# The last two token tiles of a time-mix and GELU-FFN kernel by column halves, and the first block's output projection behind its FFN

## The chip, the cores and the metric

The kernel runs on one core of a Trainium2 chip. The metric is the device time of one execution in microseconds (us). Before the change the median of 3 runs is 937.84 us (937.31 to 937.91).

## What is computed

The input x is 4 sequences of 1024 tokens with 512 channels. It is layer-normalised, and two branches work on the normalised tokens. Their results are added to x.

```python
xn = _layernorm(x, axis=-1)
# branch 1: time mix, with a running state per hidden unit (704 of them)
xx = concatenate([xn[:, 1:2, :], xn[:, :-1, :]], axis=1) - xn
k = einsum('btc,hc->bth', xn + xx * time_mix_k, Wk)
r = einsum('btc,hc->bth', xn + xx * time_mix_r, Wr)
w = exp(-exp(time_decay))
state_t = state_(t-1) * w + relu(k_t);   out_t = state_t * r_t
out = einsum('bth,ch->btc', out, Wv)
attn = (out - mean) * rsqrt(var + 1e-5) * ln_gamma + ln_beta
# branch 2: FFN, hidden size 2048, inner values rounded to float16
D = gelu(xn.astype(float16) @ W0.T + bias0).astype(float16)
E = (D @ W1.T + bias1).astype(float16)
x + attn + E
```

## The kernel before

**Tiling.** The 4096 tokens are cut into 8 blocks of 512 (`TB`), two per sequence. A block has NS = 4 token tiles of 128. The 704 hidden units of the time mix are five full chunks of 128 and one half chunk of 64. The FFN's 2048 hidden units are NN = 16 chunks of 128. The weights W0 and W1 are each held as a sum of two reduced-precision parts (w0h and w0l, and the two halves of a w1 tile), so each product with them is two matmuls.

**The stages of a block.** `full_chunks` (L398) makes, for each full chunk, the products pk and pr (L222), the state by a scan on DVE (L386) after a Relu on ACT (L384), and the gated value g (L412). `half_chunk` (L418) makes both products of the half chunk in 64x64 quarters of the array (L430, the sum called pkr), brings them to SBUF on DVE as kr (L438, L439), then Relu, scan and gh (L442). `attention_out` (L451) is the output projection: per token tile five matmuls with g (L459) and the half matmuls with gh (L470, also 64x64), all into the sums po. Its `residual` then takes statistics, normalises, and adds the residual xres, giving z (L478 to L490). It has a hook `amid`, called between the half matmuls and the second part of the full ones. `ffn` (L519) makes for each chunk n the up product pd (`up`, 8 matmuls, L529), the GELU on ACT (L537), a cast on DVE to d (L539), and the down product into the four sums pe (`down`, 8 matmuls, L545). Up products run AHEAD = 2 chunks in front of the down products. `rounded` (L508) adds bias1 to pe and rounds to float16; `finish` (L514) adds that to z and stores it.

**Order across blocks.** TensorE's order is the program's. The main loop (L603 to L646) runs the FFN of block i. The dictionary `between` names what is inserted in front of a chunk: the projection of the same block in front of chunk 0 where `within` holds (L626: the first block and the last), the layernorm of block i+1 in front of chunk 4, its transposes and mixing in front of chunk 7 or 9. Because the two up products of `waiting` come first (L570), an inserted projection stands between the up products of chunks 1 and 2. For the blocks that are not `within`, the projection stands behind the FFN, and the half chunk of the next block is made in its `amid` hook (L642). For block 1 the half chunk is made after its full chunks (L646), since the projection of block 0 is already done. The half chunk of block 0 is made ahead of the loop (L602).

**Weights and queues.** In front of the first FFN the 16 pieces of W0 are loaded through three buffers tagged "raw" and split: ACT copies the high part (L134), DVE subtracts for the low part (L135). During the first FFN the chunks of W1 take the same way through the same three buffers and are also kept in DRAM (L164); later blocks load them from there (L168). All large loads and stores are issued on SP in the order of its queue. Instructions on ACT, DVE, POOL and SP are placed by a scheduler that follows the program's priorities; a few stages fix their own order by hand (`manual_schedule`), among them the start (L294) and the end (L581).

**The end.** In the last block the last four chunks' down products are held back (`last = 4`). Token tiles 0 to 2 are then finished one after the other. The last tile's sum over the first twelve chunks is put to SBUF with the bias (`base`, L583), and the rest of its sum is made by two halves of 256 columns, each with its own PSUM sum, rounding, addition and store (`end_by_columns`, L553).

Of the kernel before, what the change touches and what calls it, by code (L numbers as in the profile page):

```python
# [8 lines left out]
F16 = mybir.dt.float16  # L9
F32 = mybir.dt.float32  # L10
# [4 lines left out]
P = 128  # L15
# [4 lines left out]
def time_mix_and_gelu_ffn(  # L20
# [26 lines left out]
    nc = tc.nc  # L47
    B, T, C = x.shape
    HID = wkT.shape[1]
    N = w0T.shape[1]  # L50
    TB = 512
    NS = TB // P
    NC = C // P
    NN = N // P
# [9 lines left out]
    def pool(name, bufs, **kw):  # L64
        return ctx.enter_context(tc.tile_pool(name=name, bufs=bufs, **kw))
# [6 lines left out]
    two = pool("two", 2)  # L72
    three = pool("three", 3)
    four = pool("four", 4)
    ps_mm = pool("ps_mm", 4, space=bass.MemoryType.PSUM)
# [55 lines left out]
    b1_sb = const.tile([P, C], F32, name="b1_sb")  # L131
# [11 lines left out]
    def load_w0(g):  # L143
        for c in range(NC):
            raw = three.tile([P, W0G], F32, tag="raw", name=f"w0raw_{g}_{c}")
            cols = slice(g * W0G, (g + 1) * W0G)
            nc.sync.dma_start(raw, w0T[c * P : (c + 1) * P, cols])
            split(w0h[c][:, cols], w0l[c][:, cols], raw)

    def load_w1(i, n):  # L150
        if i == len(blocks) - 1 and n == NN - 1:

            parts = [
                three.tile([P, C], F32R, tag="raw", name=f"w1_{i}_{n}_{p}") for p in range(2)
            ]
            for p in range(2):
                nc.sync.dma_start(parts[p].bitcast(F32), w1_dram[n][:, p, :].bitcast(F32))
            return parts
        w1 = wide.tile([P, 2, C], F32R, tag="w1", name=f"w1_{i}_{n}", bufs=3)
        if i == 0:  # L160
            raw = three.tile([P, C], F32, tag="raw", name=f"w1raw_{n}")
            nc.sync.dma_start(raw, w1T[n * P : (n + 1) * P, :])
            split(w1[:, 0, :], w1[:, 1, :], raw)
            kept = nc.sync.dma_start(w1_dram[n].bitcast(F32), w1.bitcast(F32))  # L164
            if n == NN - 1:
                state["kept"] = kept
        else:
            nc.sync.dma_start(w1.bitcast(F32), w1_dram[n].bitcast(F32))  # L168
        return [w1[:, p, :] for p in range(2)]
# [12 lines left out]
    last = const.tile([P, NC, 1], F32, name="last")  # L182
# [187 lines left out]
    def ffn_input(i, x16s):  # L370
        xf = wide.tile([P, NC, TB], F32R, tag="xf", name=f"xf_{i}")
        for c in range(NC):
            nc.vector.tensor_copy(xf[:, c, :], x16s[c])
        return xf
# [133 lines left out]
    def rounded(i, s, pe):  # L508

        e16 = four.tile([P, C], F16, tag="e16", name=f"e16_{i}_{s}")  # L510
        nc.vector.tensor_add(e16, pe, b1_sb)  # L511
        return e16

    def finish(i, s, z, e16, cols=slice(0, C)):  # L514
        b, t0 = blocks[i]
        state["added"] = nc.vector.tensor_add(z[:, cols], z[:, cols], e16)  # L516
        nc.sync.dma_start(out[b, t0 + s * P : t0 + (s + 1) * P, cols], z[:, cols])

    def ffn(i, xf, between, state):  # L519


        pe = [ps_e.tile([P, C], F32, tag="pe", name=f"pe_{i}_{s}") for s in range(NS)]

        def up(n):
            pd = ps_mm.tile([P, TB], F32, tag="mm", name=f"pd_{i}_{n}")
            cols = slice(n * P, (n + 1) * P)
            for c in range(NC):
                for w in (w0h, w0l):
                    nc.tensor.matmul(  # L529
                        pd,  # L530
                        w[c][:, cols],
                        xf[:, c, :],
                        start=(c == 0 and w is w0h),
                        stop=(c == NC - 1 and w is w0l),
                    )
            d16 = two.tile([P, TB], F16, tag="d16", name=f"d16_{i}_{n}")
            state["gelu"] = nc.scalar.activation(d16, pd, AF.Gelu, bias=b0_sb[:, n : n + 1])  # L537
            d = wide.tile([P, TB], F32R, tag="d", name=f"d_{i}_{n}", bufs=4)
            nc.vector.tensor_copy(d, d16)  # L539
            return d  # L540

        def down(n, s, d, w1, first=0, end=NN, sum_=None, cols=slice(0, C)):

            for part in range(2):
                nc.tensor.matmul(  # L545
                    pe[s] if sum_ is None else sum_,
                    d[:, s * P : (s + 1) * P],
                    w1[part][:, cols],
                    start=(n == first and part == 0),
                    stop=(n == end - 1 and part == 1),  # L550
                )

        def end_by_columns(s, chunks, z):  # L553


            first = NN - len(chunks)
            for half in range(2):
                cols = slice(half * C // 2, (half + 1) * C // 2)
                sum_ = ps_mm.tile([P, TB], F32, tag="mm", name=f"end_{half}")[:, : C // 2]
                for n, operands in chunks:  # L560
                    down(n, s, *operands, first=first, sum_=sum_, cols=cols)
                e16 = four.tile([P, C], F16, tag="e16", name=f"e16_end_{half}")[:, : C // 2]
                nc.vector.tensor_add(e16, sum_, state["base"][:, cols])  # L563
                finish(len(blocks) - 1, s, z, e16, cols)

        last = 4 if i == len(blocks) - 1 else 0
        AHEAD = 2
        waiting = [(up(n), load_w1(i, n)) for n in range(AHEAD)]  # L570
        for n in range(NN):
            if n in between:
                between[n]()
            if n + AHEAD < NN:
                waiting.append((up(n + AHEAD), load_w1(i, n + AHEAD)))
            if n < NN - last:
                operands = waiting.pop(0)
                for s in range(NS):
                    down(n, s, *operands, end=NN - last if s == NS - 1 else NN)
        if last:  # L580
            with tc.manual_schedule(engines={nc.tensor.engine, nc.vector.engine}):  # L581
                chunks = list(zip(range(NN - last, NN), waiting))
                state["base"] = two.tile([P, C], F32, tag="xx", name="base")  # L583
                nc.vector.tensor_add(state["base"], pe[NS - 1], b1_sb)
                for s in range(NS - 1):
                    for n, operands in chunks:
                        down(n, s, *operands)
                    finish(i, s, state["zs"][s], rounded(i, s, pe[s]))
                end_by_columns(NS - 1, chunks, state["zs"][NS - 1])
        return pe  # L590

    state = {}
    behind = ExitStack()
    first_x16s, xk, pks = first_inputs(x_now, behind)

    full_chunks, half_chunk = attention(0, xk, pks)
# [4 lines left out]
    for i in range(len(blocks)):  # L603
        more = i + 1 < len(blocks)
        if i == 0:
            for grp in range(N // W0G):
                load_w0(grp)
            behind.close()
            load_late_constants()
        if more:  # L610

            with tc.issue_after(state["kept"].ins) if i == 1 else nullcontext():
                x_now = load_x(i + 1)

        def out_stage():
            state["zs"] = attention_out(i, g, gh)

        def next_norm():
            with tc.issue_after(added.ins) if added else nullcontext():
                layernorm(i + 1, x_now)  # L620

        def next_inputs():
            transposed(x_now)
            state["mixed"] = mixed_inputs(i + 1, state["gelu"])

        within = i == 0 or not more  # L626
        added = state.get("added")
        between = {0: out_stage} if within else {}
        if more:
            between[4] = next_norm  # L630
            between[9 if i == 0 else 7] = next_inputs
        pe = ffn(i, xf, between, state)
        if more:
            x16s, xk = state["mixed"]
            e16s = [rounded(i, s, pe[s]) for s in range(NS)]
            xf = ffn_input(i + 1, x16s)
            full_chunks, half_chunk = attention(i + 1, xk)
            next_gh = []
            if within:
                zs = state["zs"]  # L640
            else:
                zs = attention_out(i, g, gh, lambda: next_gh.append(half_chunk()))  # L642
            for s in range(NS):
                finish(i, s, zs[s], e16s[s])
            g = full_chunks()
            gh = next_gh[0] if next_gh else half_chunk()  # L646
# [43 lines left out]
```

## The time and the profile before

| | us |
|---|---|
| median of 3 runs | 937.84 |
| profiled execution, whole | 937.6 |
| its span, first to last instruction | 935.5 |
| TensorE busy (matmul) | 930.3 |
| DVE busy | 500.7 |
| ACT busy | 164.4 |
| POOL busy | 55.6 |

The profiled execution has 9338 instructions, and the granted clock of TensorE reads 1.000. The views used are these. The first part of the page gives busy time, share of the span and number of instructions of each engine. The chain of waits in order of time follows the work that ended last back from the end; each line has a start, a length, the engine and the line of the program. The timeline of one engine shows start, length, engine, line, operation, output and inputs, how many instructions were merged, and in brackets the idle time ahead of it and what ended it. A line of the waits names who waited for whom, and then the total in us, the number of times and the longest. The table of windows gives busy time by stretches of the span.

The matmuls of the stages cost, in the chain: pd 24.9% of the span, pe 24.7%, po 14.8% (L459) and 1.6% (L470), pk 14.8%, pr 14.7%, pkr 3.0%.

### The profile page before, as it was taken

The numbers are of one execution on the slowest core, as the hardware profiler recorded it, in microseconds if no ns is written. First come the engines' busy times: TensorE is split into PE (matmuls) and PEld (weight loads), VectorE is DVE, ScalarE is ACT, GpSimd is POOL, SyncE is SP. The second block draws the span as 40 slices with busy tenths as digits, with TensorE's granted clock in tenths as the row PEclk, the third lists the DMA queues.
The fourth block names the chain that finished last, engine by engine and source line by source line (L and its number), as shares of the span: only waits on it lengthen the run. The fifth ranks groups of instructions, "written<-read, shape, count | busy, mean of one in ns | idle before, by whom it ended". The sixth has DMA issues, their size and how long they took to land.

```text
span 935.5 us, 9338 instructions
## 1 busy us (share of the span) xinstructions
PE 930.3 (99%) x3513; PEld 593.2 (63%) x3513; DVE 500.7 (54%) x875; ACT 164.4 (18%) x273; POOL 55.6 (6%) x130
## 2 busy tenths in 40 slices
PE   9999999999999999999999999999999999999998
PEld 8448854885448854588545884458844688445686
DVE  6678772833846338463484535755257552552513
ACT  5423410220002200112001220112100121001021
POOL 1010000000100001000010000100001000000100
PEclk9999999999999999999999999999999999999999
DMA  9654660443204432054320543105431044310243
GB/s 299 208 169 158 225 224 1 139 155 113 90 0 158 144 105 90 0 171 145 100 80 0 180 143 118 55 1 192 146 113 46 15 143 146 102 45 1 67 157 114
DMA packets 40296, 106.53 MB, mean 114 GB/s; under 512 B 4511, under 2 KB 5820, under 8 KB 40252
## 3 DMA queue, kind: packets, MB, share of 16 engines
q1 hardware_dynamic: 40192, 105.92, 34.1%
q8 instruction: 28, 0.46, 0.2%
q14 instruction: 16, 0.13, 0.0%
q10 hardware_dynamic: 60, 0.02, 0.0%
HBM read 89.14 MB, written 16.78 MB: 113 GB/s over the span
## 4 chain that ended last, share of the span: by engine, by line
PE 99%; DVE 0%; POOL 0%; issue 0%; POOLq 0%
PE pd L529 25%; PE pe L545 25%; PE po L459 15%; PE pk L222 15%; PE pr L222 15%; PE pkr L430 3%; PE po L470 2%; PE idle L243 1%; PE pt L261 0%; DVE z L516 0%; DVE e L511 0%; DVE e_end L563 0%; POOL ident masks.py:199 0%; PE small L300 0%; POOL ident masks.py:197 0%
## 5 line engine op out<-in xcount | busy, mean ns | idle before, releaser
L545 PE MATMUL pe<-w,d 128*128 128x512 f32 x1016 | 248.6, 389 | 0.0
L545 PEld LDWEIGHTS pe<-w,d 128*128 128x128 f32 x1016 | 190.6, 188 | 40.1 <-issue 0.4
L529 PE MATMUL pd<-xf,w0h 128*128 128x512 f32 x512 | 202.8, 396 | 0.0
L529 PE MATMUL pd<-xf,w0l 128*128 128x512 f32 x512 | 199.3, 389 | 0.0
L539 DVE CAST d<-d 128x512 fp32r<-128x512 f16 x128 | 54.2, 424 | 185.7 <-ACT d L537 184.3
L537 ACT ACTIVATE d<-pd,small_sb 128x512 f16<-128x512 f32 x128 | 87.8, 687 | 345.4 <-PE pd L529 345.4
L222 PE MATMUL pk<-xk,wk 128*128 128x512 f32 (+1 forms) x392 | 144.8, 515 | 0.0
L222 PE MATMUL pr<-xnT,wr 128*128 128x512 f32 x320 | 143.7, 592 | 0.0
L459 PE MATMUL po<-wv_sb,g 128*128 128x512 f32 x320 | 140.8, 595 | 0.0
L222 PEld LDWEIGHTS pk<-xk,wk 128*128 128x128 f32 x392 | 67.5, 190 | 70.6 <-issue 70.4
L529 PEld LDWEIGHTS pd<-xf,w0h 128*128 128x128 f32 x512 | 96.1, 188 | 23.3 <-issue 2.7
L529 PEld LDWEIGHTS pd<-xf,w0l 128*128 128x128 f32 x512 | 96.1, 188 | 21.7 <-issue 1.9
L222 PEld LDWEIGHTS pr<-xnT,wr 128*128 128x128 f32 x320 | 60.5, 189 | 76.4 <-issue 76.2
L459 PEld LDWEIGHTS po<-wv_sb,g 128*128 128x128 f32 x320 | 60.1, 190 | 76.0 <-issue 75.4
L216 DVE STREAM_TRANSPOSE xnT<-x 32x512 f32<-32x512 f32 x112 | 78.7, 702 | 2.0
L384 ACT ACTIVATE rk<-pk 128x512 f32<-128x512 f32 x40 | 23.9, 597 | 229.9 <-PE pk L222 229.4
L195 DVE BATCH_NORM_STATS2 sty<-po 128x6 f32<-128x512 f32 x32 | 22.0, 689 | 61.6 <-PE po L470 60.0
L386 DVE TENSOR_TENSOR_SCAN st<-small_sb,carry,rk 128x512 f32<-128x512 f32 (+1 forms) x24 | 30.7, 1280 | 41.9 <-ACT rk L384 41.9
L412 DVE TENSOR_TENSOR g<-st,pr 128x512 f32<-128x512 f32 x40 | 27.4, 684 | 35.3 <-PE pr L222 34.7
L386 DVE TENSOR_TENSOR_SCAN st<-small_sb,rk 128x512 f32<-128x512 f32 (+1 forms) x24 | 29.2, 1218 | 29.1 <-ACT rk L384 29.1
L189 POOL TENSOR_SCALAR ry<-mvy 128x1 f32<-128x1 f32 x32 | 11.5, 358 | 432.4 <-DVE mvy L196 432.4
L384 ACT ACTIVATE rk<-kr 64x512 f32<-64x512 f32 x8 | 5.0, 630 | 146.4 <-DVE kr L439 146.4
(70 smaller groups left out, 489.9 us busy)
## 6 DMA issues: line engine op xcount, KB each, us to landing
w<-w1d SPq DMA_DIRECT2D x111, 512.0 KB, 3.3
x<-in_L_attn_x SPq DMA_DIRECT2D x32, 256.0 KB, 3.4
xres<-in_L_attn_x SPq DMA_DIRECT2D x32, 256.0 KB, 2.7
w1d<-w SPq DMA_DIRECT2D x16, 512.0 KB, 2.9
out<-z SPq DMA_DIRECT2D x31, 256.0 KB, 2.5
w0raw<-in_L_ffn_W SPq DMA_DIRECT2D x16, 256.0 KB, 3.7
w1raw<-in_L_ffn_W SPq DMA_DIRECT2D x16, 256.0 KB, 3.4
wr<-in_L_attn_Wr SPq DMA_DIRECT2D x4, 352.0 KB, 5.3
```

What stands on the lines that cost most here:

```text
L195: nc.vector.bn_stats(st6, src)
L216: nc.vector.transpose(dst[i * Q : (i + 1) * Q, :, :, j, :], src[j * Q : (j + 1) * Q, :, :, i, :],)
L222: return nc.tensor.matmul(dst, w[c][:, cols], src, start=(c == 0), stop=(c == NC - 1))
L384: nc.scalar.activation(rk[:hw], pk, AF.Relu)
L386: nc.vector.tensor_tensor_scan(st[:hw], w_sb[:hw, h : h + 1].to_broadcast([hw, TB]), rk[:hw], 0.0 if t0 == 0 else carry[:hw, h : h + 1], A ...
L412: nc.vector.tensor_mul(g[:, h, :], st, pr)
L430: nc.tensor.matmul(out_, w[c][rows, H0:], src, start=(c == 0), stop=(c == NC - 1),)
L459: nc.tensor.matmul(pos[s], g[:, h, s * P : (s + 1) * P], wv_sb[:, h, :], start=(first and h == 0), stop=(not first and h == NF - 1),)
L529: nc.tensor.matmul(pd, w[c][:, cols], xf[:, c, :], start=(c == 0 and w is w0h), stop=(c == NC - 1 and w is w0l),)
L537: state["gelu"] = nc.scalar.activation(d16, pd, AF.Gelu, bias=b0_sb[:, n : n + 1])
L539: nc.vector.tensor_copy(d, d16)
L545: nc.tensor.matmul(pe[s] if sum_ is None else sum_, d[:, s * P : (s + 1) * P], w1[part][:, cols], start=(n == first and part == 0), stop=( ...
```

## The change

There are three edits. `within` becomes `not more`, so the projection of block 0 is no longer inserted into its FFN; it follows it, as for blocks 1 to 6, with the half chunk of block 1 in its `amid` hook. In the last block, tiles 2 and 3, and no longer tile 3 alone, get a base in SBUF and are finished by column halves. And `finish` can store its columns in several parts; tiles 0 and 1 of the last block are stored in two.

```diff
-    def finish(i, s, z, e16, cols=slice(0, C)):
+    def finish(i, s, z, e16, cols=slice(0, C), stores=1):
         b, t0 = blocks[i]
         state["added"] = nc.vector.tensor_add(z[:, cols], z[:, cols], e16)
-        nc.sync.dma_start(out[b, t0 + s * P : t0 + (s + 1) * P, cols], z[:, cols])
+        width = (cols.stop - cols.start) // stores
+        for c0 in range(cols.start, cols.stop, width):
+            part = slice(c0, c0 + width)
+            nc.sync.dma_start(out[b, t0 + s * P : t0 + (s + 1) * P, part], z[:, part])
...
-        def end_by_columns(s, chunks, z):
+        def end_by_columns(s, chunks, base, z):
...
-                nc.vector.tensor_add(e16, sum_, state["base"][:, cols])
+                nc.vector.tensor_add(e16, sum_, base[:, cols])
...
+        by_columns = range(NS // 2, NS) if last else ()
...
-                    down(n, s, *operands, end=NN - last if s == NS - 1 else NN)
+                    down(n, s, *operands, end=NN - last if s in by_columns else NN)
         if last:
             with tc.manual_schedule(engines={nc.tensor.engine, nc.vector.engine}):
                 chunks = list(zip(range(NN - last, NN), waiting))
-                state["base"] = two.tile([P, C], F32, tag="xx", name="base")
-                nc.vector.tensor_add(state["base"], pe[NS - 1], b1_sb)
-                for s in range(NS - 1):
-                    for n, operands in chunks:
-                        down(n, s, *operands)
-                    finish(i, s, state["zs"][s], rounded(i, s, pe[s]))
-                end_by_columns(NS - 1, chunks, state["zs"][NS - 1])
+                bases = {}
+                for s in by_columns:
+                    bases[s] = two.tile([P, C], F32, tag="xx", name=f"base_{s}")
+                    nc.vector.tensor_add(bases[s], pe[s], b1_sb)
+                for s in range(NS):
+                    z = state["zs"][s]
+                    if s in by_columns:
+                        end_by_columns(s, chunks, bases[s], z)
+                    else:
+                        for n, operands in chunks:
+                            down(n, s, *operands)
+                        finish(i, s, z, rounded(i, s, pe[s]), stores=2)
...
-        within = i == 0 or not more
+        within = not more
```

The scheduler reorders other engines in consequence. On DVE the layernorm of block 1 moves to between the splits of W0, and the 16 transposes of block 1's input begin between the two instructions that make kr of block 0; the projection's DVE work of block 0 moves behind the FFN. On ACT the order at the start of the first FFN stays: the splits of W0, three of W1, the Relu of the half chunk, the load of the table, the GELUs. On TensorE three up products of block 0 now stand ahead of the first down product. On SP the loads of xres for tiles 2 and 3 of block 0 move behind the FFN.

More of the change, by code (lines that the diff above doesn't have):

```diff
@@ L558, in end_by_columns @@
                 cols = slice(half * C // 2, (half + 1) * C // 2)
-                sum_ = ps_mm.tile([P, TB], F32, tag="mm", name=f"end_{half}")[:, : C // 2]
+                sum_ = ps_mm.tile([P, TB], F32, tag="mm", name=f"end_{s}_{half}")[:, : C // 2]
                 for n, operands in chunks:
                     down(n, s, *operands, first=first, sum_=sum_, cols=cols)
-                e16 = four.tile([P, C], F16, tag="e16", name=f"e16_end_{half}")[:, : C // 2]
-                nc.vector.tensor_add(e16, sum_, state["base"][:, cols])
+                e16 = four.tile([P, C], F16, tag="e16", name=f"e16_{s}_{half}")[:, : C // 2]
+                nc.vector.tensor_add(e16, sum_, base[:, cols])
                 finish(len(blocks) - 1, s, z, e16, cols)
         last = 4 if i == len(blocks) - 1 else 0
+        by_columns = range(NS // 2, NS) if last else ()
         AHEAD = 2
```

## The prediction

> **What bounds the kernel now.** I read the page's first part, then the chain of waits in order of time, then the table of windows by block, then the timelines of ACT and DVE around the first FFN, then SP's waits. The engine shares:
>
> ```profile
> PE 930.3 (99%) x3513; PEld 593.2 (63%) x3513; DVE 500.7 (54%) x875; ACT 164.4 (18%) x273; POOL 55.6 (6%) x130
> ```
>
> TensorE never rests, so the time is the sum of its matmuls: a matmul saved, or a hole opened in that row, counts in full. The chain of waits, in order of time (start, length, what):
>
> ```profile
> 1.34 4.21 PE idle L243 x18
> ...
> 7.43 2.10 PE pk L222 x18
> ...
> 43.93 3.60 PE pkr L430 x32
> 47.53 3.85 PE pd L529 x16
> 51.38 8.58 PE po L459 x20
> 59.97 1.88 PE po L470 x16
> 61.84 8.78 PE po L459 x20
> ...
> 163.00 5.66 PE pd L529 x24
> ...
> 231.94 3.44 PE pkr L430 x32
> ...
> 278.51 5.48 PE pd L529 x24
> ```
>
> See that in block 0 the projection (po) stands between the up products of chunks 0 and 1 (pd x16) and that of chunk 2: 19.24 us of matmuls (51.38 to 70.62) that need nothing of the GELU. In blocks 1 to 6 it stands behind the FFN with the next half chunk (pkr) in it, which is where the change puts block 0's. So later blocks show the price of the new order: from one first pd to the next, block 0 takes 115.47 us (47.53 to 163.00), block 1 115.51, blocks 2, 3 and 4 115.10 each (windows).
>
> What the 19.24 us cover is on the two engines that make the FFN's first operand d. ACT, then DVE, same stretch (timeline: start, length, engine, line, operation):
>
> ```profile
> 56.59 0.63 ACT L384 ACTIVATE rk<-kr 64x512 f32<-64x512 f32 x1 [2.21 <-DVE kr L439]
> 57.23 1.28 ACT L537 ACT_TABLE_LOAD   x1
> 58.53 1.27 ACT L537 ACTIVATE d<-pd,small_sb 128x512 f16<-128x512 f32 x2
> ```
>
> ```profile
> 55.02 0.68 DVE L438 COPY kr<-pkr 128x512 f32<-128x512 f32 x1
> 55.80 0.69 DVE L439 TENSOR_TENSOR kr<-kr,pkr 128x512 f32<-128x512 f32 x1
> 57.32 1.22 DVE L386 TENSOR_TENSOR_SCAN st<-small_sb,rk 64x512 f32<-64x512 f32 x1 [0.82 <-ACT rk L384]
> 58.57 0.88 DVE L442 TENSOR_TENSOR gh<-st,kr 64x256 f32<-64x256 f32 x2
> 59.55 0.76 DVE L539 CAST d<-d 128x512 fp32r<-128x512 f16 x2
> ```
>
> The first d exists at about 59.95, though its pd was done by 49.4: the GELU waits behind the half chunk's Relu on ACT, that behind kr on DVE, and kr behind the last splits of W0 and the first of W1 (the last w split runs 54.41 to 55.10). None of it shows today, because PE asks for d only at 72.46. The splits are paced by three raw buffers, which SP waits for:
>
> ```profile
> SPq L147 <- DVE w0l L135: 9.8, 13, 1.4
> ```
>
> [...] 18 matmuls of 128x128 took 4.21 us cold, the same shape and count 2.10 us at 7.43, though the clock column reads 1.00 for both. [...] pkr alone takes 3.60 us and the 24 pd behind it 5.66; beside the projection's half matmuls 3.44, and 5.48 behind full chunks.
>
> **The change part by part.** The order of the built kernels shows what moves.
>
> *Projection of block 0 moved: matmul time.* No matmul is added. pkr of block 1 goes from 3.60 to 3.44 (0.16), the pd after the projection from 1.84 to 1.81 (0.03), block 1's first pd from 5.66 to 5.48 (0.18). Block 1 also has one pe group of 2.04 instead of 1.81 us (at 186.79): its W1 chunk was issued at 181.06, behind loads of x that wait for DVE's transposes, which in block 1 stand behind the kr work at 163.03; in the new order kr comes earlier, as in blocks 2 to 6, which lack this hole. That is 0.23. Sum 0.60 us gained (bounds 0.37 to 0.60).
>
> *Its cover removed.* PE now runs three up products (pd x24, 5.66 us: 47.53 to 53.19), and then the first pe, which waits for d of chunk 0. Nothing else stands before it on PE: whatever d is late is a hole.
> How late at the least? With kr's copy at 55.02 as before, the new DVE queue is: kr copy (0.66 to its successor), one transpose of the next x (0.70), kr add (0.70): done 57.1. Then two transposes (1.40), the scan (1.15), a transpose (0.70), gh twice (0.88), the cast (0.43): 61.7. ACT keeps up (Relu 0.63, table 1.28, GELU 0.69: 59.8). The five transposes come forward because the projection's DVE work no longer precedes them. Hole at least 61.7 - 53.2 = 8.5 us.
> And kr's copy itself gets later. The layernorm of block 1 moves in front of and between the W0 splits. Its first BN_STATS stands before the second scan and the first w0l, and waits for x, whose load is issued at 21.64 and takes up to 4.7 us (issue to landing of line 86: 2.6/3.5/4.7), so until about 26, where DVE was free at 23.27. Hold 2.5 to 3.0 and 0.60 for itself: the first w0l, and so the fourth W0 load, start some 3.3 us later. One load cycle is about 3.4 (issue to cast, 37.27 to 40.69) plus 0.62 plus 0.69, and 13 W0 and 3 W1 loads go through three buffers, so there is little slack to recover in. Recovered is about 1.6 on the fourth load: it took 5.0 us (26.03 to 31.03) with the DMA engines at full share (windows), and goes out later, when they are less loaded. Lost again: three more BN_STATS (0.60), four aggregates (0.13), the wait for POOL's rstd (1.5, as at 78.92) and four normalizes (0.46), 5.7 us of DVE time, of which the idle stretches that DVE has between splits (2.76, 2.28, 1.41, 1.93, 1.31) take most. Walking the new order of DVE, ACT and SP with these durations puts the last w split at 57.9 to 58.7 instead of 55.1: 3.2 late, bounds 0 (all absorbed) and 5 (nothing recovered: 3.3 + 1.5 + a little). The first d is then at 64.8: a hole of 11.6 us, from 8.5 to 13.5.
> Behind the hole things hold: the last d of this stretch I walked, chunk 3, is due about 71.4 (after w_0_3, which waits for the first pe) and used about 77.
>
> *The clock.* [...] The row at 1.34 prices the return: 4.21 - 2.10 = 2.1 us. [...] I take 2.1; 0 if the clock stays.
>
> *Queues passed.* On SP the loads of xres 2 and 3 of block 0 move from 65.31 to behind the FFN, the form of blocks 1 to 6; xres 0 and 1 stay early. The W1 loads no longer stand behind them. POOL's rstd of block 1 goes before two carries of block 0, whose readers are far off. Both cost nothing.
>
> *Last two tiles by columns, two stores each.* Tile 2 runs 16 matmuls of 256 columns instead of 8 of 512: starts 117 ns apart in today's last tile (929.58 to 931.34, 15 steps) against 226.7/2 = 113, so +0.06 us of PE. One more base add (0.69) goes at 921.2, where DVE is idle until 923.03. Today the end is DVE's: e 0.70, z 0.69, then e_end and z twice, to 932.78, while PE ends at 931.62. With tile 2 in halves DVE is level with PE: last half at 931.68, e_end and z 0.87: 932.55. Gain 0.2. The three more stores cost SP about 0.35 each between z's that are 0.8 apart, so they hide; less data in flight at the end may give a little. Gain 0.25, bounds -0.2 (were each weight load exposed) and 0.5.
>
> **Sum:** +11.6 + 2.1 - 0.60 - 0.25 = +12.85 us. The profiled execution took 937.6 (span 935.5 and 2.1 around it), 0.24 under the median; 937.6 + 12.85 = 950.45, and with 0.24 950.7.
>
> **The rivals.**
> *A: the early layernorm is absorbed.* DVE was busy only 27.5 of the 40 us from 20 to 60 in the windows. Then the hole is 8.5: +8.5 + 2.1 - 0.85 = 9.75, 947.6. Against it: the first BN_STATS sits in front of the first split, in a loop with little slack. 0.20.
> *B: the hole without a drop of the clock.* For it: the clock column never shows one. Against: the row at 1.34. +10.75: 948.6. 0.10.
> *C: a second hole,* at the third or fourth chunk, from transposes and splits crowding DVE while PE catches up: some 3 us more, 953.7. Against: the slack of about 5 us above. 0.05.
> *D, the other side: d is there in time,* the GELU getting ahead of the half chunk's Relu. Then only the gains remain: -0.85, 937.0. It would need d by 53.2, or hole and clock together under 0.85 us. Against it: [...] kr at 55 even today. 0.03.
> *That the columns do nothing* moves any case by 0.25 only.
>
> **How the numbers follow.** Main case (hole 10 to 13.5, cold restart) 0.62: 950.7, own range 948.8 to 954. A reaches to about 946.8 with a short restart, B lies inside, C mostly inside. Range 946.8 to 954.0. Slower by over 0.2% (1.9 us, about what a measurement can tell) in all but D and its neighbourhood: 0.95; within 0.2% 0.02; faster 0.03.
>
> **What would show it.** Right: PE idle before the first pe at about 53.2 for about 11 us, released by DVE's cast of d; the next pe and pd groups 3.6 instead of 1.8 us; first BN_STATS of block 1 waiting for the x load; blocks 0 and 1 after the hole 0.6 shorter; last z 0.2 nearer to PE's end. Wrong: no gap there (D), a gap of 8.5 with kr's copy at 55 (A), groups of 1.8 right after the gap (B), a further gap at the third or fourth pe (C).

## The result, and the profile after the change

| | before | after |
|---|---|---|
| median, us | 937.66 (937.31 to 937.91, 4 runs) | 950.01 (949.79 to 950.27, 4 runs) |
| ratio, 95% interval | | 1.0132 (1.0119 to 1.0144) |
| profiled execution, us | 937.6 | 949.79 |
| its span, us | 935.5 | 948.1 |
| mean granted clock | 1.000 | 0.995 |

The median before is that of the three runs above and one more. The change costs 12.54 us of span: the trace files hold it as 935.547 and 948.089, which the page rounds to tenths. The page's engine shares of the changed kernel show that TensorE's work has not grown with it:

```profile
PE 931.6 (98%) x3521; PEld 595.4 (63%) x3521; DVE 502.4 (53%) x878; ACT 164.4 (17%) x273; POOL 54.5 (6%) x130
```

Matmul time is up by 1.3 us (930.3 before) while the span is up by 12.5, so the rest is time in which TensorE stands still. A line of its waits says where (who waited for whom, total in us, times, longest):

```profile
PE pe L548 <- DVE d L542: 11.6, 1, 11.6
```

It is one wait, and before the change there was none on this pair. The chain of waits of the changed kernel around it, in order of time (start, length, what), shows what d waited for:

```profile
49.97 2.96 DMA w0raw<-in_L_ffn_W
...
54.33 2.38 DMA w1raw<-in_L_ffn_W
...
56.73 0.63 ACT w L134
...
57.38 0.69 DVE w L135
...
58.07 0.60 DVE kr L438
...
59.21 0.64 DVE kr L439
...
61.33 1.22 DVE st L386
...
64.29 0.44 DVE d L542
...
64.77 3.61 PE pe L548 x8
68.38 1.81 PE pd L532 x8
```

Read it upwards from the pe at 64.77. It waits for the cast of d; that stands on DVE behind the half chunk's scan (st), that behind the two instructions that make kr, and these behind the split of the third W1 chunk, whose data came last. TensorE had finished its three up products at 53.2: started at 47.53, a pd x24 of 5.66 ends at 53.19, and from there to 64.77 it is 11.58. Before, the same cast ended at about 59.95, and the projection of block 0 covered the time until 72.46.

DVE's timeline of the changed kernel (start, length, line, operation, idle time ahead and its cause) shows the early part of the delay, some 30 us before the hole:

```profile
26.14 0.69 DVE L195 BATCH_NORM_STATS2 stx<-x 128x6 f32<-128x512 f32 x1 [2.79 <-DMA x<-in_L_attn_x]
...
28.79 0.69 DVE L135 TENSOR_TENSOR w0l<-w0raw,w0h 128x512 fp32r<-128x512 f32 x1
...
39.42 0.55 DVE L199 TENSOR_SCALAR x<-x,mvx,rx 128x512 f32<-128x512 f32 x1 [1.49 <-POOL rx L190]
...
57.98 0.68 DVE L438 COPY kr<-pkr 128x512 f32<-128x512 f32 x1
58.59 0.69 DVE L216 STREAM_TRANSPOSE xnT<-x 32x512 f32<-32x512 f32 x1
```

The layernorm of block 1 now stands among the splits of W0. Its first statistics wait 2.79 us for x, so the first w0l starts at 28.79 instead of 25.32, where DVE's timeline of the kernel before has it:

```profile
25.32 0.68 DVE L135 TENSOR_TENSOR w0l<-w0raw,w0h 128x512 fp32r<-128x512 f32 x1
```

The normalisation then waits 1.49 us for POOL. The copy of kr starts at 57.98 instead of 55.02, and a transpose of block 1's input already stands between it and the addition.

The table of windows of the changed kernel (columns: window, its length, busy time of PE, PEld, DVE, ACT and POOL, granted clock, DMA share, GB/s) shows the second loss:

```profile
57.50:58.00 0.50, 0.00 (x0) 0.00 (x0) 0.50 (x2) 0.00 (x0) 0.00 (x0) 0.81 0.99 401
58.00:63.00 5.00, 0.00 (x0) 0.00 (x0) 4.89 (x8) 3.03 (x4) 0.18 (x1) 0.50 0.99 360
63.00:68.00 5.00, 3.23 (x8) 2.57 (x9) 4.66 (x10) 0.84 (x2) 0.00 (x0) 0.50 0.00 0
68.00:68.50 0.50, 0.50 (x4) 0.42 (x3) 0.50 (x1) 0.08 (x1) 0.00 (x0) 0.95 0.00 0
```

The clock is at half from about 57.8 (0.81 over half a microsecond) to 68.05. The first pe group of 64.77 falls into that and takes 3.61 us instead of 1.81.

The gains are in the order of matmuls. The long chain of the changed kernel:

```profile
129.62 3.44 PE pkr L430 x32
...
176.19 5.48 PE pd L532 x24
...
291.29 5.48 PE pd L532 x24
```

pkr and the pd behind it have the short form of the later blocks, 3.44 and 5.48. Block 1 takes 291.29 - 176.19 = 115.10 us instead of 115.51. Block 0 takes 176.19 - 47.53 = 128.66, and 128.66 - 11.58 - 1.80 = 115.28 instead of 115.47. So 0.41 + 0.19 = 0.60 us are gained.

At the end, DVE's timeline of the changed kernel runs from the rounding of tile 0 to the last addition:

```profile
938.88 0.69 DVE L511 TENSOR_TENSOR e<-pe,b_sb 128x512 f16<-128x512 f32 x1 [0.82 <-PE pe L548]
...
945.00 0.42 DVE L516 TENSOR_TENSOR z<-z,e 128x256 f32<-128x256 f32 x1
```

From the first of these to the end of the last it is 6.54 us; before, it was 6.68:

```profile
926.10 0.69 DVE L511 TENSOR_TENSOR e<-pe,b_sb 128x512 f16<-128x512 f32 x1 [0.82 <-PE pe L545]
...
932.36 0.42 DVE L516 TENSOR_TENSOR z<-z,e_end 128x256 f32<-128x256 f32 x1
```

From the end of the last addition to the end of the span it is 2.67 instead of 2.77, another 0.10. This part can't be put down to the smaller stores: over the ten traces of kernels with the new end it varies from 2.57 to 2.87. Sum of the four: 11.58 + 1.80 - 0.60 - 0.24 = 12.54, the whole difference of the two spans.

### The profile page after: what moved, and what is told of

Its sections match the earlier page's. It is cut to its first block, busy times and chain, and to the rows that moved or that the text cites. A ratio compares the mean times of both kernels' runs of the same rounds, so it can differ in the third digit from the quotient of the medians.

```text
span 948.1 us, 9361 instructions
## 1 busy us (share of the span) xinstructions
PE 931.6 (98%) x3521; PEld 595.4 (63%) x3521; DVE 502.4 (53%) x878; ACT 164.4 (17%) x273; POOL 54.5 (6%) x130
## 4 chain that ended last, share of the span: by engine, by line
PE 95%; DVE 2%; DMA 2%; issue 0%; ACT 0%; POOL 0%; DVEq 0%; POOLq 0%; SPq 0%
PE pe L548 24%; PE pd L532 24%; PE po L459 15%; PE pk L222 14%; PE pr L222 13%; PE pkr L430 3%; PE po L470 2%; DMA w0raw<-in_L_ffn_W 1%; PE idle L243 1%; DVE w0l L135 0%; DVE st L386 0%; ACT w0h L134 0%; DVE z L516 0%; DMA w1raw<-in_L_ffn_W 0%; PE pt L261 0%
## 5 line engine op out<-in xcount | busy, mean ns | idle before, releaser
L548 PE MATMUL pe<-w,d 128*128 128x512 f32 x1008 | 248.4, 391 | 11.6 <-DVE d L542 11.6
```

The source lines that it names most:

```text
L548: nc.tensor.matmul(pe[s] if sum_ is None else sum_, d[:, s * P : (s + 1) * P], w1[part][:, cols], start=(n == first and part == 0), stop=( ...
```

## The experiments

The prediction's theory: each microsecond that the first d is late is one of hole; d is late because of the queues on DVE and ACT (the layernorm and transposes of block 1, then the half chunk's Relu, scan and gh), and the idle time costs TensorE its clock besides. The rivals: the end by columns or another part of the move costs the time; the loads of the weights alone pace d; the slow first group has another cause than idleness. Each experiment has its own runs of the kernel before beside it, and its ratio is to these.

**1. The end alone, and the move alone.** The first kernel takes back the move, the second makes only the move:

```diff
 end alone (against the changed kernel)
-        within = not more
+        within = i == 0 or not more
 move alone (against the kernel before)
-        within = i == 0 or not more
+        within = not more
```

> Only the end of the last block is changed (tiles 2 and 3 by columns, two stores for tiles 0 and 1); the projection of block 0 stays in its FFN. My theory: nothing but the end moves, -0.2 us in the span (935.3), from a DVE that no longer trails TensorE by the rounding and addition of tile 2. Rival: 16 more weight loads are exposed at 256 columns, +0.2 to +0.5 us. Rival: more, smaller stores at the end cost or save up to 0.5 us. All are under what a time can tell, so the end of the trace decides.

Measured: 937.34 us (936.78 to 937.68, 13 runs) against 937.72 before; ratio 0.9994 (0.9986 to 1.0003). The trace has the 6.54 us between the same two instructions as the full change.

> Only the projection of block 0 is moved behind its FFN; the end is the old one. My theory: the whole loss is here, ratio 1.013 to 1.014 (950.2 us), with the same hole of 11.6 us in front of the first down product and one group at half speed. Rival (the end has a share in the loss): nearer to 1.010.

Measured: 951.55 us (951.08 to 953.09); ratio 1.0149 (1.0135 to 1.0163). PE's timeline of the kernel with the move alone:

```profile
64.59 3.78 PE L545 MATMUL pe<-w,d 128*128 128x512 f32 x8 [10.84 <-DVE d L539]
```

All of the loss is in the move. The end saves 0.14 us between the two instructions by the trace; the times can't tell it from none. The hole is 0.7 shorter here than in the full change, but TensorE starts its first FFN 0.6 later and loses 2.37 to the clock instead of 1.80. That makes its span 0.6 longer than the changed kernel's. The median is 1.5 above it: another 0.7 lies outside the span, and three of the four executions have a lower mean clock (0.993) than the profiled one (0.995, 951.08 us).

**2. The layernorm of block 1 out of the splits.** It is tied behind a cast of d, first that of chunk 5 (the last one made when the layernorm is called), then, as shown, that of chunk 2:

```diff
-            nc.vector.tensor_copy(d, d16)
+            state.setdefault("casts", []).append(nc.vector.tensor_copy(d, d16))
...
-            with tc.issue_after(added.ins) if added else nullcontext():
+            behind = added or state["casts"][2]
+            with tc.issue_after(behind.ins):
```

> The changed kernel, with the layernorm of block 1 (and so its transposes) queued on DVE behind the cast of chunk 5 of the first FFN; everything else as changed. My theory: the splits of W0 and the half chunk return to their old times, the first d is ready at about 59.95 as in the kernel before, the hole shrinks from 11.6 to 6.8 us and the clock still drops: 4.8 us less than the changed kernel, 945.2 us. Rival A (the early layernorm costs nothing, the hole is the half chunk's alone): 950.0 us, hole 11.6. Rival (the late layernorm is missed at the end of the FFN): the hole shrinks but the start of block 1 waits, 947 us or more.

Measured for chunk 5: 950.95 us (950.43 to 951.5), where 945.2 was expected. Two groups in PE's timeline of that kernel:

```profile
59.61 3.78 PE L548 MATMUL pe<-w,d 128*128 128x512 f32 x8 [6.15 <-DVE d L542]
...
105.59 3.94 PE L548 MATMUL pe<-w,d 128*128 128x512 f32 x8 [3.17 <-DVE d L542]
```

The first hole shrank as expected, but the layernorm, transposes and mixing then came too late and crowded DVE near the end of the FFN. There the cast of d was late again: a second hole of 3.17 us, and a second slow group, 3.94 us for its eight matmuls. This is the miss that the prediction's case C describes, in another place. So the version behind chunk 2:

> The changed kernel, with one instruction order altered: the layernorm of block 1 is queued behind DVE's cast of d for chunk 2 of block 0 (about where the kernel before has it), instead of between the splits of W0. Nothing is left out. Prediction's theory (the early layernorm delays the splits by about 3 us, the relative place of the transposes causes the rest): the hole in front of the first pe shrinks from 11.6 to about 6.6 us (kr's copy at about 54.6, d's cast near 59.5), the half-clock loss behind it is 2 to 2.9, and there is no second hole at chunk 5, since the layernorm isn't as late as in the version behind chunk 5: 950.0 - 5.0 + 0.5 = about 945.5 us. If the splits' loads and not the layernorm set kr's time, the hole stays at 11 or more and the time at 949.5 to 950. If any late layernorm leaves the FFN's end too little room, a second hole of 3 us with its own slow group comes and the time is about 950.

Measured: 945.22 us (944.46 to 946.07); ratio 1.0079 (1.0065 to 1.0093). The chain of that kernel:

```profile
54.97 0.61 DVE kr L438
...
59.41 0.44 DVE d L542
...
59.89 3.78 PE pe L548 x8
63.67 2.10 PE pd L532 x8
```

The hole is 6.70 us and no second one follows. The move of the layernorm, with the transposes that follow it, was worth 4.88 us of hole: kr is copied 3.1 earlier, and 1.8 lie between kr and the cast, where the transposes stood. The clock's loss is 2.26 (3.78 and 2.10 against 1.81 each), 0.46 more than in the changed kernel. 4.88 - 0.46 = 4.42; the spans differ by 4.44.

**3. The half chunk's rest behind d.** Besides, the Relu, scan and gh of block 0's half chunk are queued behind chunk 1's GELU and cast (with `later`, the half chunk makes kr only and keeps the rest in `state["rest"]`):

```diff
-        gh = half_chunk()
+        gh = half_chunk(later=True)
...
+        def rest_of_half_chunk():
+            with tc.issue_after(state["gelu"].ins), tc.issue_after(state["cast"].ins):
+                state["rest"]()
...
+        if i == 0:
+            between[0] = rest_of_half_chunk
```

> The version with the layernorm behind the cast of chunk 2, and besides the half chunk's Relu, scan and gh of block 0 queued behind chunk 1's GELU on ACT and chunk 1's cast on DVE. Nothing is left out. Prediction's theory (d of chunk 0 waits behind the Relu on ACT and behind scan and gh on DVE): d is cast directly after kr's add, at about 57, so the hole is 3.5 to 3.8 us,[...] and the half-clock loss 0 to 2: 940.5 to 942.5 us. If the queue order of ACT and DVE behind kr isn't what holds d (for instance its table load or the W0 splits alone), the hole stays near 6.5 and the time near 945.5.

Measured: 940.38 us (939.18 to 942.12, 12 runs); ratio 1.0028 (1.0019 to 1.0036). DVE's timeline and PE's of that kernel (the profiled execution, 939.18, was the fastest of the twelve):

```profile
53.40 0.69 DVE L438 COPY kr<-pkr 128x512 f32<-128x512 f32 x1
54.19 0.69 DVE L439 TENSOR_TENSOR kr<-kr,pkr 128x512 f32<-128x512 f32 x1
54.79 0.42 DVE L548 CAST d<-d 128x512 fp32r<-128x512 f16 x1
```

```profile
55.27 2.12 PE L555 MATMUL pe<-w,d 128*128 128x512 f32 x8 [1.97 <-DVE d L548]
```

The cast stands 1.39 us behind the copy of kr instead of 4.5. The hole is 1.97, shorter than expected because the loads ran 1.5 us ahead of those in the version before; whether the edit or chance brought them forward isn't shown. TensorE keeps its clock in this execution and in four others (mean clock 1.000, 939.18 to 940.02 us). The other seven have a mean clock of 0.998 and took 940.09 to 942.12 us, so there the clock fell; how long their holes were isn't known. The median, 940.38, is not that of the execution shown.

**4. kr ahead of the last splits.** Last, the two instructions of kr go in front of the last two splits of W0 and the first of W1, and the other splits of W1 behind the first GELU (`state["kr"]` is kr's addition, `state["gelu_0"]` the first GELU):

```diff
-            split(w0h[c][:, cols], w0l[c][:, cols], raw)
+            late = g == N // W0G - 1 and c >= NC // 2
+            with tc.issue_after(state["kr"].ins) if late else nullcontext():
+                split(w0h[c][:, cols], w0l[c][:, cols], raw)
...
-            split(w1[:, 0, :], w1[:, 1, :], raw)
+            with tc.issue_after(state["gelu_0" if n else "kr"].ins):
+                split(w1[:, 0, :], w1[:, 1, :], raw)
```

> The version before this one, and besides kr's copy and add stand in front of the last two W0 splits on DVE, and the splits of W1 behind the first GELU on ACT. Nothing is left out. Prediction's theory (every us that d is late is a us of hole, and with d in time only the gains of matmul order 0.60 and of the tail 0.2 remain): hole at most 0.5 to 1, no slow group, span near 935.2, time 937.0 to 937.6 us, at or just under the kernel before. If the move had another cost besides d's lateness (pkr or po behind the FFN, other stalls), the time stays at 939 or more though the hole is gone. If W1's later splits now hold d of chunk 1 or 2 or the down products, a hole of 1 to 3 us opens at the second to fourth pe.

Measured: 937.63 us (936.65 to 938.4, 13 runs) against 937.64; ratio 0.9998 (0.999 to 1.0007). PE's timeline of that kernel:

```profile
53.05 1.98 PE L559 MATMUL pe<-w,d 128*128 128x512 f32 x8
...
82.55 2.11 PE L559 MATMUL pe<-w,d 128*128 128x512 f32 x8 [0.32 <-DVE d L552]
```

The first pe follows the up products without a gap, and the whole 12.4 us are back. No other cost of the move is left to see. Its gain doesn't show fully: at chunk 8 the cast of d stands behind a split, a transpose and a subtraction of the mixing, and block 0 takes 115.92 us instead of 115.28. The next version holds the last of the 16 transposes behind that cast:

```diff
...
-            transposed(x_now)
+            transposed(x_now, None if i else state["casts"][8])
```

> The version without a hole (937.63), and the last transpose of block 1's input, and so its mixing, held behind the cast of d for chunk 8. Nothing is left out. In the version before, pe of chunk 8 waited (0.32, and its group took 2.11 instead of 1.81) because that cast stood on DVE behind a W1 split, a transpose and a subtraction of the mixing. Prediction's theory (matmul order 0.60 and tail 0.2 are all that the change gains, once d is never late): the wait goes, block 0 takes 115.3 to 115.4 us from first pd to first pd instead of 115.92, span 934.8 to 935.0, time 937.0 to 937.2, 0.5 to 0.6 under the kernel before. If the wait only moves to the next chunk, block 0 stays at 115.9 and the time at 937.6.

Measured: 936.93 us (936.38 to 938.15, 13 runs) against 937.88; ratio 0.9991 (0.9983 to 1.0000). This is the best version found, by the ratio some 0.8 us under the kernel before, at the limit of what the runs can tell. Its trace doesn't bear out the whole expectation: the wait at chunk 8 is gone, but the first chunk and chunk 9 lose some 0.2 us each, and block 0 takes 115.71 us, not 115.3 to 115.4. The profiled span, 935.5, is that of the kernel before.

**5. The clock.** If idleness costs the clock, matmuls that keep TensorE busy in the hole must take the slow group away. The identity is multiplied with itself, and nobody uses the result:

```diff
+            if i == 0 and n == 0:
+                for _ in range(48):
+                    nc.tensor.matmul(pe[0][:, :P], ident, ident, start=True, stop=True)
```

> The changed kernel, with 48 matmuls of the identity (128x128, into a sum that the first down product overwrites) in front of the first down product of block 0: about 11.2 us of work for TensorE inside the hole, whose results are used by nobody. My theory (an idle TensorE loses its clock): the first down products run at full speed, 1.81 instead of 3.61 us, and the kernel is 1.8 us faster than the changed one: 948.2 us. Rival (the first group was slow for another reason, as operands that come late one by one): it stays at 3.6 us and the time at 950.0 us.

Measured: 950.88 us (950.66 to 951.2), so nothing was saved. PE's timeline and its waits for d:

```profile
53.11 10.88 PE L582 MATMUL pe<-ident 128*128 128x128 f32 x96
65.34 2.11 PE L548 MATMUL pe<-w,d 128*128 128x512 f32 x8 [1.35 <-DVE d L542]
```

```profile
PE pe L548 <- DVE d L542: 3.3, 2, 2.0
```

The slow group is gone, but with more matmuls in the program the scheduler placed nine transposes in a row on DVE (68.41 to 74.85), and a later d made TensorE wait 2.0 us more. The run is confounded. The next one holds DVE's order as in the changed kernel:

> The changed kernel with 48 matmuls of an identity with itself, whose results nobody uses, put in front of the first pe, and DVE's order of transposes, casts and W1 splits held as in the changed kernel, so that no second wait arises. Prediction's theory (the half-clock groups behind the hole are the price of TensorE's idleness): TensorE stays at full clock through the wait, first pe 1.8 to 2.1 us instead of 3.61, wait plus filler still 11.6 to 12.0, no wait at the fourth pe: 948.0 to 948.7 us, 1.3 to 2.0 under the changed kernel. If the slow first group comes of something else (operands, PSUM, the order of the queue), it stays at 3.6 and the time at 950 or above.

Measured: 950.04 us (948.33 to 951.59, 4 runs), inconclusive: the profiled execution, the slowest of the four, had its d 1.7 us later than the changed kernel. Its windows:

```profile
67.00:67.50 0.50, 0.50 (x3) 0.35 (x3) 0.47 (x2) 0.21 (x1) 0.00 (x0) 0.66 0.00 0
67.50:70.50 3.00, 3.00 (x9) 2.35 (x8) 2.88 (x6) 0.62 (x1) 0.00 (x0) 0.50 0.00 0
70.50:71.00 0.50, 0.50 (x4) 0.42 (x3) 0.48 (x1) 0.00 (x0) 0.00 (x0) 0.93 0.00 0
```

The filler ended at 63.82 and 2.66 us of waiting were left. The clock fell all the same, at about 67.2, 0.7 us after the first pe had begun, and came back at 70.6. By the mean clock it fell in one other execution too: the two that read 0.998 took 951.59 and 951.01 us, the two that read 0.999 and 1.000 took 948.33 and 949.07. A hole that is known better is that of experiment 2, so 28 such matmuls were put into the version with the layernorm behind chunk 2, with DVE's order held as it is there:

> The version with the layernorm behind the cast of chunk 2, and 28 matmuls of an identity with itself, whose results nobody uses, in front of the first pe of block 0; DVE's order of casts, W1 splits and transposes is held as it was without them. The filler takes about 6.35 us (48 took 10.88), from 52.8 to 59.2, against a wait of 6.7. Prediction's theory (the slow groups behind the hole are the price of TensorE's idleness): first pe and pd at 1.8 to 2.0 us instead of 3.78 and 2.10, clock column 1.00, wait plus filler still 6.5 to 7.0: 945.2 - 2.3 = about 943 us (942.7 to 943.5). If the slow groups come of something else, or the filler costs what it saves, 945 or more.

Measured: 943.18 us (942.69 to 943.36, 5 runs) against 945.22 (944.46 to 946.07) without them; ratio to the kernel before 1.0057 (1.0043 to 1.0071). The chain:

```profile
53.59 6.25 PE pe L585 x56
59.84 1.83 PE pe L551 x8
61.67 1.81 PE pd L535 x8
```

The filler fills the hole, the groups behind it take 1.83 and 1.81 instead of 3.78 and 2.10, and 2.0 us are saved where 2.3 were expected. (In this execution the cast of d ended at 59.2, so the filler outlasted the wait by some 0.6 us.) In these two versions, then, the slow groups are the price of TensorE's idleness.

## Why the prediction was right

The prediction said 950.7 us; the median is 950.01. It had the mechanism right: the wait, its place, its cause and its length. The cost of the clock came out near by luck. Point by point:

- *The hole.* Forecast 11.6, measured 11.58. Its walk holds in its parts as well: the first w0l 3.47 us later (3.3 forecast), the fourth only 1.89 later, so 1.58 recovered (1.6), 1.49 for POOL's rstd (1.5), the last of the W1 splits ahead of kr done at 58.07 (57.9 to 58.7), the first d at 64.72 (64.8). Experiments 2 to 4 take the hole away piece by piece: 4.9 us for the early layernorm and the transposes; about 3.1 for Relu, scan and gh (the cast stands 1.39 instead of 4.53 behind kr); that leaves 3.6, of which 1.5 went with the earlier loads in the trace of experiment 3, and the last 2.0 with the splits ahead of kr. With all of them moved the hole is gone.
- *The clock.* Forecast 2.1, from the row at the kernel's start; measured 1.80. That a hole would cost TensorE its clock was the author's estimate, for which the trace of before has only the slow matmuls of that row; the changed kernel's windows and experiment 5 show it. This term was mis-sized by 0.3, and that it came so near is luck. The row at the start prices a burst of 18 matmuls, all of it slow; it doesn't say how long the clock stays low behind a hole. The traces have losses from 1.80 to 2.92 behind a hole at the first pe (2.92 with the layernorm behind chunk 5: 3.78 and 2.76 against 1.81 each), and which it is depends on something the prediction didn't use, given under the hardware below. Nor does its term fit its own signs: a pe and a pd both at 3.6 would be 3.6 us of loss, and only the pe was.
- *The order of matmuls.* Forecast 0.60, measured 0.60, in the blocks where it was put.
- *The end.* Forecast 0.25, measured 0.24, of which only the 0.14 on DVE is shown (0.2 forecast); the other 0.10 lies within what that stretch varies by. The halves do cost matmul time: from the first of the held-back down products to TensorE's end it is 7.80 us instead of 7.70, so 0.10 where 0.06 was counted. The last z stands 0.92 behind TensorE's end instead of 1.16, the 0.2 nearer that was named as a sign.
- *The rest of the difference*, 0.35, lies outside the span: 2.05 us around it before, 1.70 after, 1.89 with the end alone and 2.37 with the move alone. Nothing here explains that. The median stands as far above its profiled execution after the change (0.22) as it did before (0.24).

The rivals: A (the layernorm absorbed, hole 8.5) fell, kr was copied at 57.98 and not at 55. B (no loss of clock) fell by the changed kernel's own windows, which read 0.50, and experiment 5 shows why. The column that spoke for it could not decide: the record of the clock in the trace of the kernel before begins only 6.55 us into the span, so the column reads 1.00 over the slow matmuls ahead of that. C (a second hole) didn't come in the changed kernel, where the d of chunk 3 is cast at 71.46 and used at about 77; it did come when the layernorm was put too late. D (d in time) fell: on ACT the first GELU started at 61.88, behind the half chunk's Relu at 59.94. It would have given the gains alone; the versions without a hole, at 937.63 and 936.93, are that case built on purpose, and 937.0 was its forecast.

## What to carry to other kernels

Work that keeps an engine busy while its next operand is made is cover; before you move it, walk the operand's whole path (loads, splits, each queue in order) and compare the time it is ready with the time it is asked for without the cover, and keep in mind that a scheduler will fill the space with other work. Once the operand is late, look to the order of the queues in front of it first: here edits of the queues in three steps gave back 12.4 us, while filling TensorE's wait gave back 2.0. And when you push work back to free a queue, look where it lands: the same layernorm, with its transposes, cost 4.9 us of hole when early, 3.2 and a slow group when too late, and opened no hole of its own in between.

## What the runs showed of the hardware

The clock column of the windows gives the stretch at half clock (where a window is partly at half, its share is taken from the mean). It is 57.81 to 68.05 = 10.24 us in the changed kernel, and the trace file's own record of the clock has 10.240; it is 6.83 in the version with the layernorm behind chunk 2 (57.23 to 64.06):

```profile
57.00:57.50 0.50, 0.00 (x0) 0.00 (x0) 0.32 (x1) 0.48 (x2) 0.00 (x0) 0.73 0.81 172
57.50:64.00 6.50, 4.11 (x10) 3.25 (x11) 4.94 (x11) 3.12 (x5) 0.44 (x1) 0.50 0.32 118
64.00:64.50 0.50, 0.50 (x4) 0.40 (x3) 0.14 (x1) 0.33 (x1) 0.00 (x0) 0.94 0.00 0
```

and 3.41 in the run with the filler shown above (67.16 to 70.57).

In the first two of these traces the loss follows the time from the first pe to the end of the slow stretch, and not the length of the hole. The clock column reads 0.50 there, so half of that time is an estimate of the loss: (68.05 - 64.77) / 2 = 1.64 against 1.80 measured behind a hole of 11.58; (64.06 - 59.89) / 2 = 2.09 against 2.26 behind one of only 6.70. Both fit to 0.2 us. One kernel's executions can differ in this: three of the four of that version have a mean clock of 0.996, which a stretch of 6.83 us at half gives in 943.6 us; the fourth has 0.994, nearest to what 10.24 us would give (0.9946), and is the slowest (946.07). How long its stretch was is an estimate from that mean.

After a wait of 2.66 us the clock column fell to 0.50 (the second filler run), and after one of 3.17 the group took 3.94 us (the second hole of experiment 2). After 1.97 the column stayed at 1.00 (the trace of experiment 3), and after 1.35 and 2.0 the groups took 2.11 us each (the first filler run). What decides between these cases, the length of the wait or its place in time, was not tried.
